# A graph layer with a segment maximum: layernorm's PSUM readings behind the remainder, five shared groups instead of four, 390 rows per partition

## The chip, the cores and the metric

The kernel runs on one core of one Trainium2 chip. The time is the device time of one execution in microseconds, as a median of runs. A profile of one further execution shows each engine's instructions. The engines are called PE (matrix multiplication; PEld is its weight loading), DVE (vector), ACT (activation, reads and writes elementwise), POOL (which here mostly issues gathers) and SP (which issues plain transfers). Each engine works through its own list of instructions in order.

## The reference

There are 6250 nodes with 128 features, and 206,250 edges, sorted by their destination `dst`: 100,000 random ones in both directions, and one from each node to itself.

```python
h = jnp.maximum(_layernorm(x, axis=-1), 0.0)
x_i, x_j = h[dst], h[src]
msg = jnp.concatenate([x_i, x_j - x_i], axis=-1) @ W.T + b
out = jax.ops.segment_max(msg, dst, num_segments=x.shape[0])
return x + jnp.where(jnp.isfinite(out), out, 0.0)
```

The message is a sum of a term of the destination and a term of the source: with W in two halves W1 and W2, it is h[dst] (W1 - W2) + b, plus h[src] W2. So the kernel makes two products per node, and per destination it needs the maximum of the source term over its edges.

## The kernel before

**Tables.** A node's number is l * 50 + q, with l from 0 to 124 and q from 0 to 49. The 50 sets of nodes with one q are called groups; one group is 125 rows of the source term and fits PE's rows. The layernorm stage takes two groups at a time, in 25 steps. For step k, `turn(k)` transposes the normalized rows on PE and copies them to `hT` on ACT; `product(k)` multiplies them into a PSUM tile `pm` (L544, L547) and then reads it twice on ACT: L549 writes a rounded copy to `Bp[:, 0]`, L550 writes both products to a staging area in `acc`. `remainder(k)` subtracts the rounded copy on PE in the same PSUM tile (L556) and reads what is left to `Bp[:, 1]` (L558), so that two matmuls with rounded tables give the full precision. After each fifth step the staging area is written to memory: the table `Bt` by SP (L562), and the destination's term added into the output by POOL (L563). The PSUM tiles named `pm` share two places (`ps_m`, L272), and so do the tiles that `spread_0` (L753) and `spread_a` (L766) take. A tile's place can be taken again only when the last instruction that reads it has run.

The list `micro` (L565) holds the parts of the 25 steps in order: turn k, remainder k-2, product k-1. `ln(n)` (L572) emits the next n of them; `ln_spare` emits as many as a budget of PE time allows, during the counting below.

**Which edges go where.** Each of the 128 partitions holds the edges of 49 destinations. For up to one edge per destination and group, the maximum is taken by one-hot matmuls on PE: the main loop. Groups of the order 41 to 0 have one place per destination. Four pairs of groups are shared: a pair has two places per destination (`MG = 4`), and each place costs two chunks, one of each group of the pair, since the edge in it may come from either. There are 50 places, 8 of them with two chunks: 58 chunks for every tile of destinations. Edges that find no place are the rest: they are compacted to a list per partition, and their rows are gathered from `Bt`, one row for all 128 partitions at a time, GR = 396 rows. A partition with too many hands some to the next one (up to 136); if that isn't enough a flag is set, and a branch at the end goes through all edges one by one (L1188).

**The stage ahead of the loop.** DVE compares each edge with up to 41 neighbours to count its place (L636; PE adds the comparisons up in the PSUM tile `dup`), until 88 us. ACT turns the counts to signs (L721), DVE sums them (L743), and eleven passes of conditional copies (`pass_`, L779, called in L855) compact the list. After pass i the functions in `rest[i]` are emitted. They are: `spread_0` and `spread_a`, by which the partitions' counts go through PE (L754), DVE (L758 to L764) and PE again (L768), and `spread_b`, in which DVE reads the outcome (L772 to L777); what is left of layernorm, `ln(30)` ahead of the passes and the rest after pass 0; `names()`, which reads `dup` on ACT in four pieces (L737) and makes a second operand (L738); `turned()`, which transposes three tables by PE into `dup` and casts them by ACT (L796), each in two parts of 8 and 6 blocks; `clear_early`, two memsets on POOL (L835) in the space of the staging area; and after pass 7 the first gathers and the first one-hots (`build`, L205).

**The main loop.** 13 tiles of destinations (12 of 490, one of 392) by 25 pairs of places: 325 steps. In each, PE makes z for the next pair (L990), ACT turns z to one-hots (L991), PE multiplies them with both tables of `Bp` (L1127, two matmuls a chunk), and DVE takes the maximum (L1134 in a tile's first step, L1136 in the others). Three PSUM tiles hold z, two hold the products. The order of the pairs is made in L977: 8 of the 25 have a place with two chunks. Between, DVE takes in the gathered rows (`stream_step`, L172) and builds the one-hots of later tiles (L205, L209, L212). When a row is due is set by `fill_in` (L1040): GR rows over 291 steps by time estimates of each engine. POOL issues a gather (L92) for each row, up to 36 rows ahead. After the last row the remaining rows of each destination are gathered and merged (L1096 to L1101), in the last 34 steps.

Of the kernel before, what the change touches and what calls it, by code (L numbers as in the profile page):

```python
# [14 lines left out]
AF = mybir.ActivationFunctionType  # L15
# [4 lines left out]
P = 128  # L20
# [9 lines left out]
WIN = 1792  # L30
NBLK = WIN // P
# [4 lines left out]
OV = 136  # L36
GR = 396
R0 = 32
# [7 lines left out]
CNT = 12  # L46
MG = 4
SQ = 64
# [9 lines left out]
def gnn_kernel(tc, x, src, dst, W, b, out):  # L58
# [20 lines left out]
    A_ = nc.scalar  # L79
    T_ = nc.tensor  # L80
# [20 lines left out]
    with ExitStack() as ctx:  # L101
# [14 lines left out]
        with ExitStack() as body:  # L116
            body.enter_context(tc.manual_schedule())
            keep = body.enter_context(tc.tile_pool(name="keep", bufs=1))
            identb = keep.tile([P, P], BF16, name="identb")
# [148 lines left out]
            with ExitStack() as pre:  # L268
# [269 lines left out]
                def where(k):  # L538
                    g, o = divmod(2 * k, GQ)
                    return g % 2, o  # L540

                def product(k):
                    pm = steps[k]["pm"] = ps_m.tile([P, 2, 2 * C], F32, name="pm")
                    T_.matmul(pm[:L], bsel, brow.rearrange("k (o c) -> k o c", o=1).to_broadcast([P, 2, 2 * C]),  # L544
                              start=True, stop=False)
                    for j in range(2):
                        T_.matmul(pm[:L, j], hT[k % 2][:, j, :L], wT, start=False, stop=j == 1)  # L547
                    g, o = where(k)
                    A_.copy(Bp[:L, 0, 2 * k:2 * k + 2], pm[:L, :, :C])  # L549
                    A_.copy(stage[:, g, :, o:o + 2].rearrange("l b q c -> l q b c"),  # L550
                            pm[:L].rearrange("l q (b c) -> l q b c", b=2))
# [14 lines left out]
                for k in range(NP_ + 2):  # L566
                    for f, n in ((turn, k), (remainder, k - 2), (product, k - 1)):
                        if 0 <= n < NP_:
                            micro.append((n if f is turn else -1, lambda f=f, n=n: f(n),
                                          {turn: 0.25, product: 1.15, remainder: 0.13}[f]))  # L570

# [150 lines left out]
                dups = s16.bitcast(BF16)  # L722
                ln(30)
                for r in range(2):
# [8 lines left out]

                def names():
                    for a in range(0, WIN, 512):
                        z = min(a + 512, WIN)
                        A_.copy(dups[:, a:z], dup[:, a:z])  # L737
                    A_.activation(name, q16, AF.Abs)  # L738

# [49 lines left out]

                def turned(t, *todo):  # L790
                    pt = dup.rearrange("p (j l) -> p j l", l=P)
                    for a, z in ((0, 8), (8, NBLK)):
                        for j in range(a, z):
                            for m, (e, w) in enumerate(todo):
                                T_.matmul(pt[:, j], e[:, j * P:(j + 1) * P], w, start=m == 0, stop=m == len(todo) - 1)
                        A_.copy(t[:, :, a:z], pt[:, a:z].rearrange("p j l -> p l j"))  # L796

# [45 lines left out]
                rest = {i: [] for i in range(12)}  # L843
                rest[0] += [spread_0, lambda: ln(len(micro)), names]
                rest[1] += [lambda: turned(TD, (dlc, identb))]
                rest[2] += [spread_a, lambda: turned(TV, (vm, identb), (low, negL))]
                rest[3] += [lambda: turned(TQ, (dups, sgI), (name, halfI))]
                rest[4] += [spread_b]
                rest[5] += [clear_early, load_first]
# [51 lines left out]
            with ExitStack() as main:  # L901
# [74 lines left out]
                for k in range(Q // 2):  # L976
                    order.append([twos.pop(0) if k % 3 == 1 and twos else ones_.pop(0), ones_.pop(0)])  # L977
                assert not twos and not ones_
# [279 lines left out]
```

## Time and profile before

| | us |
|---|---|
| median of 3 runs (777.7 to 780.37) | 779.11 |
| the profiled execution | 781.03 |
| its span, from the first to the last instruction | 779.3 |
| DVE busy in the span | 703.4 |
| PE busy in the span | 684.6 |
| ACT busy in the span | 553.7 |
| POOL busy in the span | 489.7 |
| PE's granted clock, mean | 0.964 |

A row of the profile's timeline has the start in us from the span's start, the duration, engine, line, operation, and the tile written `<-` those read; `xN` stands for N instructions merged to one row. In brackets is how long the engine was idle ahead of it and what ended that. Matmuls overlap, so that the spacing of their starts, and not the mean duration, tells what one costs. A table by stretches gives the busy time of each engine in a part of the span, and PE's granted clock as a share of full speed.

### The profile page before, as it was taken

The numbers are of one execution on the slowest core, as the hardware profiler recorded it, in microseconds if no ns is written. First come the engines' busy times: TensorE is split into PE (matmuls) and PEld (weight loads), VectorE is DVE, ScalarE is ACT, GpSimd is POOL, SyncE is SP. The second block draws the span as 40 slices with busy tenths as digits, with TensorE's granted clock in tenths as the row PEclk, the third lists the DMA queues.
The fourth block names the chain that finished last, engine by engine and source line by source line (L and its number), as shares of the span: only waits on it lengthen the run. The fifth ranks groups of instructions, "written<-read, shape, count | busy, mean of one in ns | idle before, by whom it ended". The sixth has DMA issues, their size and how long they took to land.

```text
span 779.3 us, 12126 instructions
## 1 busy us (share of the span) xinstructions
PE 684.6 (88%) x3776; PEld 517.3 (66%) x3782; DVE 703.4 (90%) x1256; ACT 553.7 (71%) x1162; POOL 489.7 (63%) x519
## 2 busy tenths in 40 slices
PE   0689875678999999999899999999999999989995
PEld 0345454556677676777667777777777777767894
DVE  7999965988999899999999999999999999886885
ACT  4689455275978879888686766868676686855863
POOL 4000011577777777777777777777777777775472
PEclk9999997579999999999999999999999999999998
DMA  6843054023433333433343333334333343332137
GB/s 194 263 100 65 2 116 97 18 82 94 109 107 91 103 111 93 122 92 112 84 119 96 103 110 97 109 107 112 100 105 108 89 125 92 109 103 81 40 77 141
DMA packets 79651, 79.40 MB, mean 102 GB/s; under 512 B 10042, under 2 KB 68495, under 8 KB 79579
## 3 DMA queue, kind: packets, MB, share of 16 engines
q0 software_dynamic: 16560, 37.64, 19.2%
q1 hardware_dynamic: 62667, 40.30, 17.9%
q10 hardware_dynamic: 352, 0.61, 0.3%
q8 instruction: 31, 0.51, 0.3%
q14 instruction: 41, 0.34, 0.1%
HBM read 39.25 MB, written 39.19 MB: 101 GB/s over the span
## 4 chain that ended last, share of the span: by engine, by line
PE 43%; DVE 20%; ACT 17%; issue 10%; DMA 7%; POOL 2%; SPq 0%; DVEq 0%; POOLq 0%; ACTq 0%
PE ps L1127 22%; PE z L990 10%; ACT oh L991 9%; DVE acc L1136 6%; PE pv L244 6%; DMA X<-Bt,ridx 5%; DVE T L636 3%; DVE X L172 3%; ACT Vb L259 2%; PE pm L547 1%; ACT Vf L259 1%; ACT dump L1166 1%; DVE dwin L673 1%; ACT acc L550 1%; POOL X L92 1%
## 5 line engine op out<-in xcount | busy, mean ns | idle before, releaser
L92 POOL DMA_INDIRECT X<-Bt,ridx x396 | 409.6, 1034 | 128.3 <-issue 37.8
L991 ACT ACTIVATE oh<-z 126x490 fp32r<-126x490 f32 (+1 forms) x754 | 380.9, 575 | 146.4 <-PE z L990 143.5
L1127 PE MATMUL ps<-oh,Bp 126*128 126x490 f32 (+1 forms) x1508 | 445.4, 423 | 10.0 <-DVE acc L1136 9.7
L1136 DVE TENSOR_TENSOR acc<-acc,ps 128x980 f32<-128x980 f32 (+1 forms) x312 | 360.1, 1154 | 39.9 <-PE ps L1127 35.5
L1127 PEld LDWEIGHTS ps<-oh,Bp 126*128 126x128 f32 x1508 | 286.0, 192 | 87.0 <-DVE acc L1136 19.2
L990 PE MATMUL z<-Vb,Sel 128*126 128x490 f16 (+1 forms) x650 | 198.0, 373 | 13.8 <-ACT oh L991 7.7
L172 DVE SCALAR_TENSOR_TENSOR X<-X,slim 128x128 f32<-128x128 f32 x395 | 136.1, 345 | 4.0 <-issue 2.4
L990 PEld LDWEIGHTS <-Sel 128*126 128x126 f16 x754 | 99.7, 140 | 48.3 <-issue 14.9
L244 PEld LDWEIGHTS <-OHQ 128*128 128x128 bf16 x840 | 58.7, 161 | 23.2 <-issue 22.5
L563 POOL DMA_DIRECT2D out_x<-acc x10 | 8.8, 1016 | 101.8 <-ACT hT L530 70.2
L244 PE MATMUL pv<-OHD,OHQ 128*128 128x28 bf16 (+1 forms) x826 | 62.0, 228 | 9.5 <-DVE OHD L212 9.5
L92 POOL DMA_INDIRECT R<-M,last_e x49 | 48.0, 980 | 22.3 <-issue 11.3
L205 DVE TENSOR_TENSOR OHQ<-T,IQ 128x1092 bf16<-128x1092 bf16 (+5 forms) x96 | 57.4, 601 | 0.2 <-DVE badc L898 0.2
L990 PE MATMUL z<-Vf,Sel 128*126 128x490 f16 (+1 forms) x104 | 38.7, 373 | 0.5 <-ACT Vf L259 0.5
L625 PE MATMUL dup<-T,identb 128*128 128x512 bf16 (+1 forms) x159 | 36.7, 357 | 2.1 <-DVE T L636 1.0
L1166 ACT ACTIVATE dump<-lane_dl,nbias 128x472 bf16<-128x472 int32 x50 | 35.2, 704 | 0.1
L625 PEld LDWEIGHTS <-identb 128*128 128x128 bf16 x164 | 16.1, 99 | 19.2 <-issue 5.1
L547 PE MATMUL pm<-wT,hT 128*125 128x256 f32 x100 | 26.5, 388 | 0.0
L673 DVE COPY_PREDICATED dwin<-big,dwin 128x472 int32<-128x472 int32 (+10 forms) x12 | 21.9, 1826 | 0.4
L549 ACT CAST Bp<-pm 125x256 fp32r<-125x256 f32 x25 | 9.3, 371 | 18.0 <-PE pm L547 17.8
L636 DVE TENSOR_TENSOR T<-KA,KB 128x1792 bf16<-128x1792 int16 x21 | 21.1, 1081 | 0.0
L547 PEld LDWEIGHTS pm<-wT,hT 128*125 128x125 f32 x100 | 19.3, 193 | 2.7
(301 smaller groups left out, 503.4 us busy)
## 6 DMA issues: line engine op xcount, KB each, us to landing
M<-X SPq DMA_DIRECT2D x66, 384.0 KB
X<-Bt,ridx POOLq DMA_INDIRECT x396
X<-in_x SPq DMA_DIRECT2D x5, 560.0 KB
out_x<-X SPq DMA_DIRECT2D x5, 560.0 KB
Bt<-acc SPq DMA_DIRECT2D x5, 560.0 KB
out_x<-acc POOLq DMA_DIRECT2D x5, 560.0 KB
ownb<-Bt SPq DMA_DIRECT2D x11, 245.0 KB
out_x<-R POOLq DMA_DIRECT2D x5, 480.0 KB
```

Source lines behind the costliest of these rows:

```text
L92: i = G_.indirect_dma_start(out=o, out_offset=None, in_=table, in_offset=bass.IndirectOffsetOnAxis(ap=idx, axis=0))
L172: step = V.scalar_tensor_tensor(G[:, j], state["prev"], slim[:, k:k + 1], G[:, j], op0=ALU.min, op1=ALU.max)
L205: return V.tensor_tensor(OHQ[:, :nl, a:z], over(TQ, z - a), iq, ALU.is_equal)
L244: last = T_.matmul(o, w, m, start=False, stop=True, skip_group_check=True)
L547: T_.matmul(pm[:L, j], hT[k % 2][:, j, :L], wT, start=False, stop=j == 1)
L625: T_.matmul(dup[:, a:z], w, e[:, a:z], start=first, stop=last)
L636: V.tensor_tensor(e, KA[:, 64:], i1, ALU.is_equal)
L990: T_.matmul(z[:L + 1, :n], Sel[:, order[i // 2][j]], f[t % 2][:, :n], start=True, stop=True)
L991: A_.activation(oh[:, :n], z[:L + 1, :n], AF.Relu)
L1127: T_.matmul(ps[:, j, :n], w, o[:, :n], start=m == 0, stop=m == len(todo) - 1)
L1136: V.tensor_tensor(a, a, ps[:, :, :n], ALU.max)
L1166: A_.activation(dump, lane_dl, AF.Sign, scale=2.0, bias=nbias[:, c:c + 1], accum_out=ends[:, c:c + 1])
```

## The change

It has three parts.

1. `product(k)` keeps only its matmuls. Its two ACT readings become `copies(k)`. The order in `micro` is now turn k, product k-1, remainder k-2, copies k-1, with the same budget for a step.
2. What layernorm has left after the counting is emitted in other places. Ahead of the passes there are 16 parts instead of 30; after pass 0 `spread_0`, then 20 parts, with the four pieces of `dups` and `name` behind each four of them; after pass 1 `spread_a`, then the rest in fours, with the first four of the six halves of `turned` behind them; the last two halves come after pass 2, `spread_b` after pass 3 (before: pass 4, and `spread_a` after pass 2).
3. Five pairs of groups are shared (`MG = 5`): 10 of 50 places have two chunks, 60 chunks for each tile; pairs k with k % 5 of 1 or 3 get them. GR falls from 396 to 390.

```diff
-GR = 396
+GR = 390
-MG = 4
+MG = 5
...
                     for j in range(2):
                         T_.matmul(pm[:L, j], hT[k % 2][:, j, :L], wT, start=False, stop=j == 1)
+
+                def copies(k):
+                    pm = steps[k]["pm"]
                     g, o = where(k)
                     A_.copy(Bp[:L, 0, 2 * k:2 * k + 2], pm[:L, :, :C])
...
-                    for f, n in ((turn, k), (remainder, k - 2), (product, k - 1)):
+                    for f, n in ((turn, k), (product, k - 1), (remainder, k - 2), (copies, k - 1)):
                         if 0 <= n < NP_:
                             micro.append((n if f is turn else -1, lambda f=f, n=n: f(n),
-                                          {turn: 0.25, product: 1.15, remainder: 0.13}[f]))
+                                          {turn: 0.25, product: 1.15, remainder: 0.13, copies: 0.0}[f]))
...
-                ln(30)
...
-                def names():
-                    for a in range(0, WIN, 512):
-                        z = min(a + 512, WIN)
-                        A_.copy(dups[:, a:z], dup[:, a:z])
-                    A_.activation(name, q16, AF.Abs)
+                def kept(a):
+                    z = min(a + 512, WIN)
+                    A_.copy(dups[:, a:z], dup[:, a:z])
+
+                def rest_of(cycles, *ops):
+                    for i in range(cycles):
+                        ln(4)
+                        if i < len(ops):
+                            ops[i]()
+
+                rest_of(4)
...
-                def turned(t, *todo):
+                def turned(t, h, *todo):
                     pt = dup.rearrange("p (j l) -> p j l", l=P)
-                    for a, z in ((0, 8), (8, NBLK)):
-                        for j in range(a, z):
+                    a, z = ((0, 8), (8, NBLK))[h]
+                    for j in range(a, z):
...
-                rest[0] += [spread_0, lambda: ln(len(micro)), names]
-                rest[1] += [lambda: turned(TD, (dlc, identb))]
-                rest[2] += [spread_a, lambda: turned(TV, (vm, identb), (low, negL))]
-                rest[3] += [lambda: turned(TQ, (dups, sgI), (name, halfI))]
-                rest[4] += [spread_b]
+                both = [(t, h, todo) for t, todo in ((TD, ((dlc, identb),)), (TV, ((vm, identb), (low, negL))),
+                                                     (TQ, ((dups, sgI), (name, halfI)))) for h in (0, 1)]
+                rest[0] += [spread_0, lambda: rest_of(5, *[lambda a=a: kept(a) for a in range(0, WIN, 512)],
+                                                      lambda: A_.activation(name, q16, AF.Abs))]
+                rest[1] += [spread_a, lambda: rest_of(-(-len(micro) // 4), *[lambda t=t, h=h, todo=todo: turned(t, h, *todo)
+                                                                            for t, h, todo in both[:4]])]
+                rest[2] += [lambda t=t, h=h, todo=todo: turned(t, h, *todo) for t, h, todo in both[4:]]
+                rest[3] += [spread_b]
...
-                    order.append([twos.pop(0) if k % 3 == 1 and twos else ones_.pop(0), ones_.pop(0)])
+                    order.append([twos.pop(0) if k % 5 in (1, 3) and twos else ones_.pop(0), ones_.pop(0)])
```

More of the change, by code (lines that the diff above doesn't have):

```diff
@@ L788, in pass_ @@
                     return step
-                def turned(t, *todo):
+                def turned(t, h, *todo):
                     pt = dup.rearrange("p (j l) -> p j l", l=P)
-                    for a, z in ((0, 8), (8, NBLK)):
-                        for j in range(a, z):
-                            for m, (e, w) in enumerate(todo):
-                                T_.matmul(pt[:, j], e[:, j * P:(j + 1) * P], w, start=m == 0, stop=m == len(todo) - 1)
-                        A_.copy(t[:, :, a:z], pt[:, a:z].rearrange("p j l -> p l j"))
+                    a, z = ((0, 8), (8, NBLK))[h]
+                    for j in range(a, z):
+                        for m, (e, w) in enumerate(todo):
+                            T_.matmul(pt[:, j], e[:, j * P:(j + 1) * P], w, start=m == 0, stop=m == len(todo) - 1)
+                    A_.copy(t[:, :, a:z], pt[:, a:z].rearrange("p j l -> p l j"))
                 own_n = pool.tile([P, 4], F32, name="own_n")
```

## The prediction

> **What bounds the kernel now.** I read the page first, for the size of each kind of work: columns are line, engine, operation, count, busy us, mean ns of one, then idle time before it.
>
> ```profile
> span 779.3 us, 12126 instructions
> ...
> L92 POOL DMA_INDIRECT X<-Bt,ridx x396 | 409.6, 1034 | 128.3 <-issue 37.8
> L991 ACT ACTIVATE oh<-z 126x490 fp32r<-126x490 f32 (+1 forms) x754 | 380.9, 575 | 146.4 <-PE z L990 143.5
> L1127 PE MATMUL ps<-oh,Bp 126*128 126x490 f32 (+1 forms) x1508 | 445.4, 423 | 10.0 <-DVE acc L1136 9.7
> L1136 DVE TENSOR_TENSOR acc<-acc,ps 128x980 f32<-128x980 f32 (+1 forms) x312 | 360.1, 1154 | 39.9 <-PE ps L1127 35.5
> ```
>
> Then the table by stretches (length, then busy us of PE, PEld, DVE, ACT, POOL; clock; DMA), one row for the layernorm stretch and one for three tiles of the main loop, and the first instruction of DVE in tiles 6, 9, 10 and 11.
>
> ```profile
> 89.20:125.20 36.00, 24.16 (x112) 17.37 (x111) 25.70 (x27) 22.22 (x56) 4.04 (x5) 1.00 0.36 73
> ...
> 457.40:595.30 137.90, 132.74 (x752) 102.63 (x751) 132.23 (x218) 99.53 (x195) 106.21 (x105) 1.00 0.38 105
> ```
>
> ```profile
> 455.68 1.18 DVE L1134 TENSOR_TENSOR acc<-ps,acc 128x980 f32<-128x980 f32 x1
> ...
> 593.66 1.18 DVE L1134 TENSOR_TENSOR acc<-ps,acc 128x980 f32<-128x980 f32 x1
> ...
> 639.35 1.18 DVE L1134 TENSOR_TENSOR acc<-ps,acc 128x980 f32<-128x980 f32 x1
> ...
> 687.52 1.18 DVE L1134 TENSOR_TENSOR acc<-ps,acc 128x980 f32<-128x980 f32 x1
> ```
>
> The main loop is bound by PE and DVE together: of 137.9 us PE idles 5.2 and DVE 5.7, in turns. Three tiles take 137.98 us, 46.0 each; tile 10 takes 48.17. Before the loop another thing rules. The timeline of DVE:
>
> ```profile
> 104.01 1.09 DVE L672 TENSOR_SCALAR big<-dwin 128x1788 int32<-128x1788 int32 x1
> ...
> 114.83 0.28 DVE L758 TENSOR_SCALAR rows<-pm 1x128 f32<-1x128 f32 x1 [7.41 <-PE pm L754]
> ...
> 116.65 1.07 DVE L672 TENSOR_SCALAR big<-dwin 128x1784 int32<-128x1784 int32 x1
> ...
> 131.83 0.16 DVE L772 CAST cols__105<-pm 128x1 int32<-128x1 f32 x1 [8.45 <-PE pm L768]
> ...
> 142.81 2.55 DVE L205 TENSOR_TENSOR acc<-T,IQ 128x1092 bf16<-128x1092 bf16 x4 [0.22 <-issue]
> ```
>
> DVE, which has the compaction passes to do, stands still for 7.41 and 8.45 us because two small matmuls (L754, L768) are queued on PE behind layernorm rounds. The chain of waits shows one such round, and the timeline of ACT its third reading:
>
> ```profile
> 94.66 0.38 PE pm L556
> 95.04 0.23 PE pm L544
> 95.27 0.88 PE pm L547 x4
> 96.17 0.23 ACT Bp L549
> 96.44 0.60 ACT acc L550
> ...
> 97.09 0.39 PE pm L556
> ```
>
> ```profile
> 95.08 0.37 ACT L558 CAST Bp<-pm 125x256 fp32r<-125x256 f32 x1 [0.20 <-PE pm L556]
> ```
>
> A round takes 97.09 - 94.66 = 2.43 us; the remainder matmul L556 waits for the readings L549 and L550 of the product just before it. Fourteen rounds run behind 89.2.
>
> **Layernorm's order, and its places (first part of the change).** The new order on PE is turn, product, remainder; the remainder of step k-2 now waits for readings made a round earlier. What is late next: the product needs the PSUM tile of two steps back, free when that step's L558 has ended. From product to product that is 1.11 (L544, L547) + 0.42 (L556 to L558) + 0.37 + 0.04 = 1.94 us; ACT's four readings, some 1.5 us, fit. Gain 0.49 a round, if nothing else enters.
>
> The places enter. The tile of L754 takes one of the two PSUM tiles. One product is always unread at that point, so the next product gets the tile of L754, and that is given back by DVE's L758, behind pass 1. PE therefore stops from about 98 until DVE has done two passes:
>
> - Four rounds end at 97.3; L754 runs at 97.6.
> - L758 comes at 104.0 (where 104.01 starts pass 2 now) and no longer waits. Its group takes 1.82, as from 114.83 to 116.65.
> - PE goes on at 104.3: five rounds, one or two at half clock (below), to 115.6; then L768, to 116.6. ACT's readings of dups and name (rows below) lie between: a quarter of 1.85 in each of four rounds' slack, the 1.74 beside L768.
> - DVE does passes 2 and 3 until 112.7, waits 4.0 for L768, then 0.6 for its group; passes 4 to 7 end at 130.6 (5 to 7 fill 132.4 to 142.4 now, 3.3 each).
> - PE starts the last five rounds at 117.1, with four of the six turned halves among them; each half adds a cast of 0.8 to 1.0 on ACT (L796), so a round takes 2.4 to 3. Last readings at 130.0, last two halves at 134.
>
> ```profile
> 125.23 1.85 ACT L737 CAST s<-dup 128x512 bf16<-128x512 f32 x4
> 126.93 1.74 ACT L738 ACTIVATE d<-q 128x1792 bf16<-128x1792 bf16 x1
> ...
> 141.51 0.81 ACT L796 CAST T<-dup 128x768 bf16<-128x768 f32 x1 [1.52 <-PE dup L795]
> ```
>
> So L205 starts at 134.1 and not at 142.81: **-8.7 us**. Of 15.9 us of waits some 4 stay, and 3.4 become a wait for the last cast (141.51 now, just ahead of L205). SP's writes of the table Bt move with the readings, and POOL is queued behind a memset:
>
> ```profile
> 124.78 1.66 POOL L563 DMA_DIRECT2D out_x<-acc  x2 [11.23 <-ACT acc L550]
> ...
> 134.24 0.75 POOL L835 MEMSET acc<- 128x784 bf16 x1 [6.71 <-DMA out_x<-acc]
> 142.87 1.62 POOL L92 DMA_INDIRECT X<-Bt,ridx  x1 [7.88 <-DVE ridx L828]
> ```
>
> ```profile
> 124.52 0.76 SPq L562 DMA_DIRECT2D Bt<-acc  x2
> 128.07 0.32 SPq L838 DMA_DIRECT2D swin<-Bt  x1
> ```
>
> The memset comes 9.5 us behind the last transfer's issue, which moves from 124.8 to 130.1; the first gather can start at 140.4, 2.4 us earlier. SP's last write of Bt, issued at 130.0, is in by 133.6, since L838, which reads it, starts 3.6 behind it now: it holds up nobody. The order during the counting, ahead of 88, I cost at nothing: DVE is busy there without a break. If that cover were gone, PE has the same 0.49 a round to give, not to lose.
>
> The clock must be watched. Two windows of the table by stretches:
>
> ```profile
> 121.74:125.15 3.41, 1.86 (x7) 1.26 (x8) 1.64 (x1) 1.74 (x5) 0.37 (x1) 1.00 0.00 0
> 125.15:128.56 3.41, 1.01 (x8) 0.85 (x8) 0.00 (x0) 3.41 (x7) 2.38 (x3) 0.50 0.94 218
> ```
>
> PE busy for 55% of a stretch of 3.4 us is followed by a granted clock of 0.50. The pause from 98 to 104 holds nearly two such stretches, so the first round behind it runs slowly; I have put in 1.3 us. [...]
>
> **Two more chunks in each tile.** 13 tiles get 60 chunks for 58: 26 more L990, 26 more L991, 52 more L1127. PE's price is its pitch, not the 423 ns:
>
> ```profile
> 337.27 1.05 PE L244 MATMUL pv<-OHD,OHQ 128*128 128x28 bf16 x14
> ...
> 340.12 0.58 PE L990 MATMUL z<-Vb,Sel 128*126 128x490 f16 x2
> ...
> 340.36 1.69 PE L1127 MATMUL ps<-oh,Bp 126*128 126x490 f32 x6
> ...
> 341.89 0.58 PE L990 MATMUL z<-Vb,Sel 128*126 128x490 f16 x2
> ```
>
> Eight matmuls from 340.12 to 341.89: 0.22 each, 0.66 a chunk, 1.3 us a tile, 17 us in all. Per tile PE has 174 x 0.22 = 38.3, five groups like that of 337.27 (5.2 at most), under 1 for the rest: 44 of 46.0. So 2 us of slack meets 1.3 us of work. Bounds: 0 (all of it fits) and 1.3 (none). Slack that comes in turns is not all usable; I take 0.5 in tiles 1 to 10, 0.7 in tile 0, and the whole price in the last two, where rows end and PE alone is the bound (1.3, and 1.0 for 392 columns): **+8.0**. ACT's 26 x 0.575 = 15 us lie in its idle 146. [...]
>
> **Six rows less.** POOL is full: gathers follow one another at 1.25 us, and near the end DVE waits for them:
>
> ```profile
> 689.76 0.94 POOL L92 DMA_INDIRECT X<-Bt,ridx  x1 [0.31 <-DMA X<-Bt,ridx]
> ...
> 691.00 0.94 POOL L92 DMA_INDIRECT X<-Bt,ridx  x1 [0.30 <-DMA X<-Bt,ridx]
> ```
>
> ```profile
> 682.82 0.35 DVE L172 SCALAR_TENSOR_TENSOR X<-X,slim 128x128 f32<-128x128 f32 x1 [2.37 <-issue]
> ```
>
> DVE saves 6 x 0.35 = 2 us, spread over the tiles and already in the 0.5. The wait of 2.37 is why tile 10 takes 2.2 us over the usual 46.0, and some 1 us more is lost behind it. POOL's chain shortens by 6 x 1.25 + 2.4 = 9.9; the loop reaches the last row about 5 to 6 earlier, so gathers are no longer last: **-3** (0 to -4).
>
> **Sum:** -8.7 + 8.0 - 3 = -3.7. The profiled execution took 781.03 (its span 779.3 and 1.7 around it), 1.9 above the median of 779.11; the sum gives 777.3 there and 775.4 for the median.
>
> **The rivals.**
> - *PE is the bound in every tile.* The price of 17 us is paid in full from the first tile on, because the slack is of a kind that a third chunk cannot use: -8.7 + 16.6 - 3 = +4.9, 784.0, slower. It decides once less than about 0.6 us a tile is hidden. For it: PE busy 96%; against it: DVE busy as much, and the pitch leaves 2 us.
> - *The pause costs the clock.* PE stays at 0.50 over four or five rounds and the turned halves (a round then about 3.2 instead of 1.94, so 4 to 5 us): sum near +0.5, 779.5. For it: 0.50 from 125 on. [...]
> - *No pause.* The tile of L754 does not hold up the next product. Rounds run through; casts and passes both end near 127: -15 + 8 - 3, 769.
> - *The change lacks rows.* If 390 were too few, the test would send the kernel into its edge-by-edge branch, far slower. Counting random edges (32 per dst, 50 groups) five groups of two hold 7 rows per partition more than four, so the margin grows by one: 0.02.
>
> **How the numbers follow.** Forecast 0.45, PE bound 0.20, clock 0.23, no pause 0.10, lack 0.02. A measurement of this kernel tells 0.3% (2.3 us) from no change. The forecast's own spread (gain 6 to 11, chunks 5 to 11) leaves a little of it within 0.3%, and the clock case lies mostly there: faster 0.54, same 0.26, slower 0.20. The likeliest is 775.4; the range takes in both outer cases with a price, 768.5 to 784.0.
>
> **What would show it.** L758 without a wait near 104; PE idle from 98 to 104 with 0.50 behind it; L772 waiting about 4; L205 at 134; first gather at 140; a usual tile of 46.5; no wait of L172 near 683. Wrong would be a tile of 47 or more, an L205 later than 138, or PE without that pause.

## The result, and the profile after

| | before | after |
|---|---|---|
| median, us | 778.75 (777.7 to 780.37) | 769.24 (768.03 to 770.2) |
| ratio, 95% interval | | 0.9873 [0.9858, 0.9888] |
| span of the profiled execution, us | 779.3 | 767.7 |
| end of the first accumulation of the loop, us | 166.8 | 160.4 |
| from there to the last accumulation, us | 604.0 | 599.0 |

The change made the kernel 1.3% faster, 9.5 us; 3.7 had been forecast. The sign and the range (768.5 to 784.0) hold the result, the size doesn't. The loop was to be 5 us longer and is 5 us shorter. Between the line numbers of before and after lie 3 from L549 on, 8 around L760 and 11 in the loop: L1127 is now L1138, L1136 is L1147.

The page of after, the groups that answer to those shown of before:

```profile
span 767.7 us, 12292 instructions
...
L92 POOL DMA_INDIRECT X<-Bt,ridx x390 | 393.2, 1008 | 118.7 <-DMA X<-Bt,ridx 37.8
...
L1138 PE MATMUL ps<-oh,Bp 126*128 126x490 f32 (+1 forms) x1560 | 454.6, 420 | 2.6 <-DVE acc L1147 2.6
...
L1147 DVE TENSOR_TENSOR acc<-acc,ps 128x980 f32<-128x980 f32 (+1 forms) x312 | 360.0, 1154 | 42.4 <-PE ps L1138 39.5
...
L172 DVE SCALAR_TENSOR_TENSOR X<-X,slim 128x128 f32<-128x128 f32 x389 | 133.9, 344 | 0.0
```

PE's products L1138 are 52 more and cost 9 us more of busy time, but the idle time ahead of them fell from 10.0 to 2.6, and the row steps at L172 wait for nothing any more.

Its timeline ahead of the loop, PE, then DVE:

```profile
99.90 0.38 PE L762 MATMUL pm<-ident,nres 128*1 128x128 f32 x2 [0.25 <-ACT Bp L561]
106.20 0.79 PE L544 MATMUL pm<-brow,bsel 128*125 128x512 f32 x1 [5.92 <-DVE rows L766]
```

```profile
105.88 0.26 DVE L766 TENSOR_SCALAR rows<-pm 1x128 f32<-1x128 f32 x1
...
118.12 0.16 DVE L780 CAST cols__105<-pm 128x1 int32<-128x1 f32 x1 [3.65 <-PE pm L776]
...
136.09 1.36 DVE L205 TENSOR_TENSOR acc<-T,IQ 128x1092 bf16<-128x1092 bf16 x2 [3.80 <-ACT T L804]
```

The reader is to see the three things that the prediction named, each 1 to 2 us late: PE stands still for 5.9 us because the small product L762 holds one of the two places of `pm` until DVE comes to L766; DVE's two waits of 7.41 and 8.45 us are now none and one of 3.65; and L205, which opens the loop's work, starts at 136.1 instead of 142.81.

The loop, in the table by stretches (length, then busy us of PE, PEld, DVE, ACT, POOL; clock; DMA), tiles 6 to 8 and tile 10, first of before, then of after:

```profile
456.90:594.80 137.90, 132.74 (x752) 102.63 (x751) 132.23 (x218) 99.53 (x195) 106.12 (x105) 1.00 0.38 105
640.50:688.70 48.20, 45.11 (x245) 34.42 (x243) 44.11 (x74) 33.19 (x65) 37.09 (x37) 0.96 0.37 105
```

```profile
451.10:587.40 136.30, 135.50 (x770) 105.95 (x769) 131.32 (x217) 102.33 (x201) 104.61 (x104) 1.00 0.38 106
632.90:678.30 45.40, 45.13 (x260) 35.33 (x259) 43.81 (x73) 34.11 (x67) 34.78 (x35) 1.00 0.39 110
```

Three tiles hold 18 more matmuls, PE is busy 2.8 us longer, and yet they are 1.6 us shorter: of 5.2 us in which PE stood idle, 0.8 are left. Tile 10 is 2.8 us shorter. The waits between 400 and 665 us (total, count, longest), before and then after, name what PE no longer waits for:

```profile
PEld ps L1127 <- DVE acc L1136: 9.1, 12, 1.2
...
PE pv L244 <- DVE OHD L212: 4.9, 6, 0.9
PE ps L1127 <- DVE acc L1136: 4.5, 9, 0.7
```

```profile
PEld ps L1138 <- DVE acc L1147: 2.2, 7, 0.9
...
PE ps L1138 <- DVE acc L1147: 0.5, 1, 0.5
```

### The profile page after: what moved, and what is told of

It reads as the page before. It is cut to its first block, busy times and chain, and to the rows that moved or that the text cites. A ratio compares the mean times of both kernels' runs of the same rounds, so it can differ in the third digit from the quotient of the medians.

```text
span 767.7 us, 12292 instructions
## 1 busy us (share of the span) xinstructions
PE 692.2 (90%) x3860; PEld 527.1 (69%) x3860; DVE 699.8 (91%) x1250; ACT 564.7 (74%) x1188; POOL 474.4 (62%) x513
## 4 chain that ended last, share of the span: by engine, by line
PE 59%; ACT 19%; DVE 14%; issue 4%; DMA 3%; SPq 0%; DVEq 0%; ACTq 0%; POOLq 0%; POOL 0%
PE ps L1138 32%; PE z L1001 15%; ACT oh L1002 11%; PE pv L244 6%; DVE T L639 3%; ACT Vf L259 2%; DMA X<-Bt,ridx 2%; ACT Vb L259 2%; DVE acc L1147 2%; PE pm L547 1%; DVE stats L402 1%; ACT dump L1177 1%; DVE dwin L676 1%; DMA T<-in_dst 1%; PE pv L1107 1%
## 5 line engine op out<-in xcount | busy, mean ns | idle before, releaser
L1002 ACT ACTIVATE oh<-z 126x490 fp32r<-126x490 f32 (+1 forms) x780 | 393.6, 575 | 129.4 <-PE z L1001 126.0
L92 POOL DMA_INDIRECT X<-Bt,ridx x390 | 393.2, 1008 | 118.7 <-DMA X<-Bt,ridx 37.8
L1138 PE MATMUL ps<-oh,Bp 126*128 126x490 f32 (+1 forms) x1560 | 454.6, 420 | 2.6 <-DVE acc L1147 2.6
L1147 DVE TENSOR_TENSOR acc<-acc,ps 128x980 f32<-128x980 f32 (+1 forms) x312 | 360.0, 1154 | 42.4 <-PE ps L1138 39.5
L1138 PEld LDWEIGHTS ps<-oh,Bp 126*128 126x128 f32 x1560 | 295.1, 191 | 74.5 <-issue 8.6
L1001 PE MATMUL z<-Vb,Sel 128*126 128x490 f16 (+1 forms) x650 | 196.0, 370 | 14.8 <-ACT oh L1002 8.4
L1001 PEld LDWEIGHTS <-Sel 128*126 128x126 f16 x780 | 102.9, 139 | 53.0 <-issue 17.8
L172 DVE SCALAR_TENSOR_TENSOR X<-X,slim 128x128 f32<-128x128 f32 x389 | 133.9, 344 | 0.0
L205 DVE TENSOR_TENSOR OHQ<-T,IQ 128x1092 bf16<-128x1092 bf16 (+5 forms) x96 | 57.2, 599 | 0.2 <-DVE badc L909 0.2
L1001 PE MATMUL z<-Vf,Sel 128*126 128x490 f16 (+1 forms) x130 | 49.0, 377 | 0.5 <-ACT Vf L259 0.5
L547 PE MATMUL pm<-wT,hT 128*125 128x256 f32 x100 | 28.3, 409 | 0.0
L544 PE MATMUL pm<-brow,bsel 128*125 128x512 f32 x25 | 13.2, 528 | 11.1 <-DVE rows L766 5.9
```

Source lines behind the costliest of these rows:

```text
L92: i = G_.indirect_dma_start(out=o, out_offset=None, in_=table, in_offset=bass.IndirectOffsetOnAxis(ap=idx, axis=0))
L172: step = V.scalar_tensor_tensor(G[:, j], state["prev"], slim[:, k:k + 1], G[:, j], op0=ALU.min, op1=ALU.max)
L205: return V.tensor_tensor(OHQ[:, :nl, a:z], over(TQ, z - a), iq, ALU.is_equal)
L1001: T_.matmul(z[:L + 1, :n], Sel[:, order[i // 2][j]], f[t % 2][:, :n], start=True, stop=True)
L1002: A_.activation(oh[:, :n], z[:L + 1, :n], AF.Relu)
L1138: T_.matmul(ps[:, j, :n], w, o[:, :n], start=m == 0, stop=m == len(todo) - 1)
```

## The experiments

Eighteen runs of ten kernels. "Two-chunk pairs" are the loop's steps that have a place with two chunks. Tiles are counted from 0; their lengths run from one tile's last accumulation to the next one's. "Loop" runs from the first accumulation's end to the last one's, in the profiled execution. Ratios go against the kernel before on the same chip.

| kernel | median us | ratio, 95% interval | L205 at | first accumulation | tiles 5 to 9, mean | tile 10 | tile 11 | loop |
|---|---|---|---|---|---|---|---|---|
| before | 778.75 | | 142.8 | 166.8 | 45.9 | 48.2 | 47.6 | 604.0 |
| after | 769.24 | 0.9873 [0.9858, 0.9888] | 136.1 | 160.4 | 45.4 | 45.4 | 45.3 | 599.0 |
| after again | 769.32 | 0.9872 [0.9846, 0.9898] | 135.6 | 159.9 | 45.4 | 45.5 | 45.4 | 597.3 |
| layernorm part alone | 777.86 | 0.9969 [0.9951, 0.9987] | 134.4 | 158.7 | 45.9 | 50.9 | 48.0 | 608.4 |
| loop part alone | 777.83 | 0.9979 [0.9963, 0.9995] | 143.6 | 167.6 | 45.4 | 45.4 | 45.4 | 599.8 |
| loop part, 396 rows | 778.17 | 0.9990 [0.9967, 1.0012] | 143.0 | 167.0 | 45.4 | 45.5 | 45.3 | 601.1 |
| after, spread's tiles in the tile `dup` | 776.65 | 0.9959 [0.9936, 0.9982] | 141.4 | 165.4 | 45.4 | 45.5 | 45.3 | 599.7 |
| after, pairs side by side | 777.05 | 0.9953 [0.9934, 0.9972] | 135.3 | 159.5 | 46.1 | 46.2 | 44.9 | 606.5 |
| layernorm part, other places for eight pairs | 771.03 | 0.9879 [0.9843, 0.9914] | 135.0 | 159.6 | 44.8 | 52.6 | 46.7 | 601.7 |
| after, L766 earlier, other places for ten pairs | 762.89 | 0.9779 [0.9748, 0.9811] | 131.7 | 156.2 | 45.5 | 45.4 | 44.4 | 596.1 |

**390 rows without the fifth group** (the kernel before, with one line of the change).

```diff
-GR = 396
+GR = 390
```

> 390 rows alone, with four shared pairs. Supply theory: the wait for gathers near 683 goes and tile 10 falls from 48.2 to 46: 775 to 776, other tiles as before. If rows held the whole loop and not its end: every tile shorter by 0.5, 771 to 773.

316,049.67 us, and both theories miss: the flag was set and the branch at the end went through all edges one by one (its step, L1208, ran 206,250 times). So the rival "the change lacks rows" describes a real mechanism, and the six rows can only go together with the fifth group; the parts of 390 rows were not to be had alone.

**The layernorm part alone** (the changed kernel with these lines of before):

```diff
-GR = 390
+GR = 396
-MG = 5
+MG = 4
-                    order.append([twos.pop(0) if k % 5 in (1, 3) and twos else ones_.pop(0), ones_.pop(0)])
+                    order.append([twos.pop(0) if k % 3 == 1 and twos else ones_.pop(0), ones_.pop(0)])
```

> The changed kernel with parts of 396 rows, four groups of two chunks and their old order: the layernorm part of the change alone. Absorbing theory: the part ahead of the loop gains what it gains in the changed kernel (L205's first cast at 136 to 138 us instead of 142.8, first accumulation 6.4 us earlier), and a tile still takes 45.7 to 46.5 us, since nothing of the loop is changed: 772 to 774 us, ratio 0.991 to 0.994. Supply theory: the loop before is held by the gathers, whose first starts only 0.9 us earlier; without the six rows the head start is lost again later, as waits of L172 or longer tiles: 776 to 779. Clock theory on the 2.3 us later end of the counting: if the wait of the one-hot cast at L658 for PE near 55 us with a half clock in the window before it comes back, it belongs to the order of the readings; if the count ends near 90.6 us, it was the phase of the clock's windows.

777.86 us, 0.9969. The start came, more of it than in after: the first accumulation 8.1 us earlier (158.7 against 166.8). The loop gave 4.4 back, 2.7 of it in tile 10, which takes 50.9 us, since gathered rows are late (another 1.2 are in tile 0, for which no cause is shown). The timeline of DVE in tile 10 has three waits that aren't in before, beside the one of 2.33 us that before has too (2.37):

```profile
646.48 0.35 DVE L172 SCALAR_TENSOR_TENSOR X<-X,slim 128x128 f32<-128x128 f32 x1 [0.61 <-DMA X<-Bt,ridx]
666.40 0.35 DVE L172 SCALAR_TENSOR_TENSOR X<-X,slim 128x128 f32<-128x128 f32 x1 [0.98 <-DVE acc L1147]
669.30 0.35 DVE L172 SCALAR_TENSOR_TENSOR X<-X,slim 128x128 f32<-128x128 f32 x1 [1.47 <-DMA X<-Bt,ridx]
```

The loop starts 8 us earlier, the first gather only 2.5 us earlier (140.4 against 142.9), so the rows' reserve shrinks by the difference. The supply theory holds for this part alone.

**The loop part alone, and the same with 396 rows** (before, with the changed lines the other way round; the second without the change of GR):

> The kernel before with parts of 390 rows, five groups of two chunks and the new order of pairs: the loop's part alone. Absorbing theory: the two extra chunks of a tile go into PE's 1.6 us of idle time, and the six rows less take some 0.4 us a tile off DVE, so a usual tile takes 45.4 us with PE idle for 0.3 us of it, and the loop is 4 to 6 us shorter: 773 to 776 us, ratio 0.993 to 0.996. Price theory (0.66 us a chunk and three us for the rows): 783 to 785, ratio 1.006. Supply theory: as much of the gain as the rows bring, 2 to 4 us.

> The kernel before with five groups of two chunks and the new order, parts of 396 rows kept: the chunks alone. Absorbing theory: PE's 1.6 us of idle time a tile take the 1.3 us of extra products, DVE's work is the same and its edge is not: 45.7 to 46.1 us a tile, 778 to 782 us, ratio 1.000 to 1.004. Price theory: 0.66 us a chunk, 8 us in all: 786 to 788, ratio 1.010 or more. Order theory: if the even spacing of the two-chunk pairs is what took the idle time out, this kernel is faster than before even with 396 rows: 774 to 777.

777.83 (0.9979) and 778.17 us (0.9990). The first has the tile and the loop of the absorbing theory (45.4 us, 4.2 us shorter), but its time lies 1.8 above the range. With 396 rows the usual tile is 45.4 us, just as in after, so the chunks and their places did it and not the rows. The price theory falls: with 26 chunks more the loop was 2.9 us shorter, and with six rows less 1.3 more (601.1 to 599.8). The time fits the absorbing theory and not the order theory (774 to 777), but the tile went lower than the absorbing theory had (45.7 to 46.1), which left the order open. The page's group of L172, before, then the layernorm part alone, then this kernel with 396 rows, shows where tiles 10 and 11 gained:

```profile
L172 DVE SCALAR_TENSOR_TENSOR X<-X,slim 128x128 f32<-128x128 f32 x395 | 136.1, 345 | 4.0 <-issue 2.4
```

```profile
L172 DVE SCALAR_TENSOR_TENSOR X<-X,slim 128x128 f32<-128x128 f32 x395 | 136.8, 346 | 6.6 <-DMA X<-Bt,ridx 3.2
```

```profile
L172 DVE SCALAR_TENSOR_TENSOR X<-X,slim 128x128 f32<-128x128 f32 x395 | 136.9, 347 | 0.0
```

With all 396 rows the waits for them are gone: the last gather is issued at 701.8 instead of 711.0. The page's group of the gathers in this kernel shows where that time comes from:

```profile
L92 POOL DMA_INDIRECT X<-Bt,ridx x396 | 398.6, 1007 | 128.4 <-issue 35.3
```

The same 396 gathers took 409.6 us in before (1034 ns each), so they are 11.0 us shorter in sum, enough for the 9.2 by which the last one comes earlier. Why a gather gets shorter I haven't found; the program's plan of when rows are due is made with the chunks' times, and was not changed by itself.

**The changed kernel once more**, beside the kernel that is told of next:

> The changed kernel once more. Two halves theory: the early start alone lost 6 us again in the loop, where rows came late in tiles 10 and 11, and the chunks and rows alone began late; together the early start is kept: 768 to 770 us, ratio 0.986 to 0.989. Chip theory: the first result was better by its chip; 772 to 776, near the product of the two single ratios (0.995). The first cast of L205 is at 136 if L658 waits for PE near 55 us again (the phase of the clock's windows), at 134 if not.

769.32 us, 0.9872, the first result again. L205 starts at 135.6, between the two values expected: L658 waits only 0.18 us here, but the counting itself began 0.8 us later than in the first profile. The two parts alone would make 0.9969 x 0.9979 = 0.9948; together they make 0.9872, 6 us more. Of these, 4.4 are what the loop gave back in the layernorm part alone; for the 2.7 of tile 10 it is the rows' reserve that the loop part brings that lets the earlier start last. The rest is near the scatter of these executions (below).

**Where the two-chunk pairs lie.** Eight pairs, no chunk added, against the layernorm part alone:

```diff
-                    order.append([twos.pop(0) if k % 3 == 1 and twos else ones_.pop(0), ones_.pop(0)])
+                    order.append([twos.pop(0) if k % 3 == 0 and twos else ones_.pop(0), ones_.pop(0)])
```

> The layernorm part alone (396 rows, four groups of two chunks), with its eight two-chunk pairs at the first, fourth, seventh place of a tile and so on, instead of the second, fifth, eighth. Spacing theory: PE's two waits in a tile, at the first and the thirteenth pair, meet two-chunk pairs now and go; PE's idle time falls from 1.6 to under 0.8 us and a tile takes 44.4 to 45.1 us, less than with five groups (45.45). Work theory: PE's 44.0 us and DVE's 43.8 are too near each other, the waits appear at other pairs, and a tile takes 45.5 to 46.2, as in the layernorm part alone (45.7).

771.03 us, 0.9879. The spacing theory holds in the tiles, which the first accumulation of tile 6 and of tile 9 show, first in the layernorm part alone (137.99 us apart), then here (134.69):

```profile
448.77 1.18 DVE L1145 TENSOR_TENSOR acc<-ps,acc 128x980 f32<-128x980 f32 x1
...
586.76 1.18 DVE L1145 TENSOR_TENSOR acc<-ps,acc 128x980 f32<-128x980 f32 x1
```

```profile
446.00 1.18 DVE L1145 TENSOR_TENSOR acc<-ps,acc 128x980 f32<-128x980 f32 x1
...
580.69 1.18 DVE L1145 TENSOR_TENSOR acc<-ps,acc 128x980 f32<-128x980 f32 x1
```

```profile
447.20:581.90 134.70, 132.22 (x753) 102.77 (x752) 131.66 (x217) 98.93 (x195) 103.29 (x104) 1.00 0.39 106
626.70:679.20 52.50, 45.34 (x237) 33.50 (x235) 44.47 (x73) 32.94 (x65) 40.22 (x41) 0.97 0.37 101
```

The same work, 132.2 us of PE and 131.7 of DVE, fits into 134.7 us instead of 138.0, 1.1 a tile. The program plans DVE's row steps by the order of the pairs, so that they move too: "places" means both, and no run parts them. The gathers are shorter here too (1010 ns against 1025, the last one issued at 699.9 instead of 705.7), with four groups: so that isn't the fifth group's alone. The second row is tile 10: 52.5 us, 7.7 more than a usual one, since L172 waits for rows; on this kernel's page:

```profile
L172 DVE SCALAR_TENSOR_TENSOR X<-X,slim 128x128 f32<-128x128 f32 x395 | 135.9, 344 | 6.9 <-DMA X<-Bt,ridx 3.6
```

The faster the tiles, the sooner the rows run out. Even so this kernel, without a fifth group, is within a few us of the changed one: 771.03 against 769.32 on one chip.

Ten pairs, side by side, against the changed kernel:

```diff
-                    order.append([twos.pop(0) if k % 5 in (1, 3) and twos else ones_.pop(0), ones_.pop(0)])
+                    order.append([twos.pop(0) if k % 5 in (1, 2) and twos else ones_.pop(0), ones_.pop(0)])
```

> The changed kernel with the two two-chunk pairs of every five side by side (second and third). Work theory: 45.4 to 45.6 us a tile, 768 to 771 us. Spacing theory: PE's idle time over 1 us a tile, 46.2 us a tile or more, 776 us or more.

777.05 us, 0.9953: the time of the spacing theory, not its sign. A tile takes 46.1, and PE idles only 0.45 us of it; instead its busy time is longer for the same number of matmuls. Tiles 6 to 8, the changed kernel run again and this one:

```profile
448.80:585.20 136.40, 135.64 (x772) 106.00 (x771) 131.43 (x217) 102.37 (x201) 104.39 (x106) 1.00 0.39 106
```

```profile
454.10:592.40 138.30, 136.96 (x771) 105.61 (x770) 132.36 (x216) 102.56 (x201) 106.02 (x106) 1.00 0.39 105
```

DVE idles 5.9 us in three tiles instead of 5.0. So places decide with ten pairs too, by 0.7 us a tile; what delays PE's matmuls within its busy time there stays open.

**The pause of PE.** The changed kernel, with the spread's two small tiles in columns added behind those of `dup`:

```diff
-                dup = ps_d.tile([P, WIN], F32, name="dup")
+                dup = ps_d.tile([P, 2048], F32, name="dup")
-                    spread["n"] = ps_m.tile([P, 512], F32, name="pm")
+                    spread["n"] = dup[:, WIN:]
-                    p = spread["c"] = ps_m.tile([P, 512], F32, name="pm")
+                    p = spread["c"] = dup[:, WIN + P:]
```

> The changed kernel, with the two small tiles of the spread (row counts and columns) in the spare end of the bank of dup instead of one of the two places that the products of layernorm use. Place theory: PE's pause of 5.9 us before the product at 106 us goes, with the half clock behind it; the last cast of L205 moves from 136 to 129 to 132, and the time falls by 3 to 6 us from that of the changed kernel: 763 to 766 us. Supply theory: the first gather stays near 142 and the loop, held by the gathers at first, gives the time back: 768 to 770. Dependency rival: the spread's products wait for the readers of dup instead, and nothing is gained: 768 to 771.

776.65 us: the dependency rival, and dearer than it had said. PE's pause is gone, but the timeline of DVE has another wait:

```profile
127.43 0.16 DVE L780 CAST cols__105<-dup 128x1 int32<-128x1 f32 x1 [10.89 <-ACT T L804]
...
141.36 2.55 DVE L205 TENSOR_TENSOR acc<-T,IQ 128x1092 bf16<-128x1092 bf16 x4 [0.19 <-issue]
```

L780 now waits 10.89 us until ACT has cast the last half of the last table out of `dup` (L804, 126.59 to 127.40), and with it stand the passes. This cast reads other columns of `dup` than L780. What L780 reads comes from the products L776, whose last operand was written by 109.8 (L772, 109.57 and 0.22); the profile names L804 and not L776 as what ended the wait. Whether the dependency is kept for the whole tile `dup` or for a part of it, no run tells.

The other way is to shorten the time that the place is held: DVE's steps L766 to L772 one pass earlier, the second products where they were. It ran undisturbed only together with other places for the ten pairs (first and third of every five):

```diff
+                def spread_c():
                     p = spread["c"] = ps_m.tile([P, 512], F32, name="pm")
...
-                rest[0] += [spread_0, lambda: rest_of(5, *[lambda a=a: kept(a) for a in range(0, WIN, 512)],
+                rest[0] += [spread_0, spread_a, lambda: rest_of(5, *[lambda a=a: kept(a) for a in range(0, WIN, 512)],
...
-                rest[1] += [spread_a, lambda: rest_of(-(-len(micro) // 4), *[lambda t=t, h=h, todo=todo: turned(t, h, *todo)
+                rest[1] += [spread_c, lambda: rest_of(-(-len(micro) // 4), *[lambda t=t, h=h, todo=todo: turned(t, h, *todo)
...
-                    order.append([twos.pop(0) if k % 5 in (1, 3) and twos else ones_.pop(0), ones_.pop(0)])
+                    order.append([twos.pop(0) if k % 5 in (0, 2) and twos else ones_.pop(0), ones_.pop(0)])
```

> The changed kernel with the vector steps of the spread's first part one pass earlier, and the two-chunk pairs at the first and third place of every five. Place theory: L205's first cast at 131 to 133 instead of 135 to 136; work theory: tiles 5 to 10 stay at 45.2 to 45.5 us, tiles 1 to 4 fall by up to 0.7 each: 763 to 766 us, ratio 0.979 to 0.983. Row rival: tiles 10 and 11 wait for rows (L172 idle over 2 us): 768 to 770.

762.89 us, 0.9779: below both kernels. The timeline of PE, and that of DVE (here L780 is L781):

```profile
101.85 0.50 PE L544 MATMUL pm<-brow,bsel 128*125 128x512 f32 x1 [2.62 <-DVE rows L766]
```

```profile
101.53 0.26 DVE L766 TENSOR_SCALAR rows<-pm 1x128 f32<-1x128 f32 x1
...
113.79 0.16 DVE L781 CAST cols__105<-pm 128x1 int32<-128x1 f32 x1 [0.20 <-PE pm L777]
131.67 1.96 DVE L205 TENSOR_TENSOR acc<-T,IQ 128x1092 bf16<-128x1092 bf16 x3 [3.72 <-ACT T L805]
```

The pause is 2.6 us, DVE's wait for the second products has gone too, and L205 comes 4 us earlier than in after. The other places brought nothing in tiles 5 to 9 (45.5 us), as the work theory said, and 47.5 in tiles 1 to 3, against 47.6; tiles 0 and 11 are shorter (47.3 and 44.4). So most of the gain is the start's, and the rows kept up.

**Runs that tell nothing of these theories.** Ten of the eighteen runs stand in three groups in which every kernel, the one before too (965.2, 957.99 and 968.92 us), took 23 to 24% longer than elsewhere, with engines waiting for nothing that the trace shows. An example is PE's weight loads at L1001 (us in total, times, longest), first in the changed kernel there, then in its first profile:

```profile
PEld L1001 <- issue: 108.6, 86, 11.9
```

```profile
PEld L1001 <- issue: 17.8, 26, 3.1
```

A kernel's own runs differ by 1 to 5% there, and the effects looked for are below 2%. So no theory is judged by these ratios; all kernels but two were run again, as told above. The one with 390 rows alone, told first, belongs to the first group; its 316,049 us don't hang on a per cent. The others are these, with the edits shown above.

The layernorm part alone, first run:

> Layernorm's part alone: the new order and the new places, with four shared pairs and 396 rows. Supply theory (gathers set when the rows end, near 711 to 718, whatever comes ahead of the loop): the loop starts some 6 us earlier, but the first gather only 1 us earlier, so most of the gain is lost at the last rows: 775 to 777 where before has 779. Stage theory (what is won ahead of the loop stays won): 772 to 773.

1.0012 [0.9914, 1.011]. The loop part alone:

> The loop's part alone: five shared pairs, their order, 390 rows, old layernorm. Slack theory (the two chunks of a tile fit into PE's idle 5 us of 138, the rows relieve the end): 774 to 776, tiles of 45.4. Price theory (a chunk costs its 0.66 us, the gain lies elsewhere): 779 to 784, tiles of 46.5.

1.0132 [1.004, 1.0224]. The loop part with 396 rows:

> Five shared pairs and their order alone, with 396 rows. Slack theory: usual tiles 45.4 to 46.0, the end held by the gathers as before: 777 to 780. Price theory: 26 chunks of 0.66 us, half to all of it: 785 to 793.

1.0205 [1.0105, 1.0305]. The changed kernel:

> The changed kernel once more, beside the next three. Two halves theory: the early start alone (776.1 us of span) lost 6 us again in the loop, where rows came late in the eleventh and twelfth tile, and the chunks and rows alone (775.7) began late; only together is the early start kept, so 768 to 770 us, ratio 0.986 to 0.989, well below the product of the two ratios (0.9969 by 0.9979, 0.995). Chip theory: the first result is that of another chip; here 774 to 777. The wait of L658 for PE near 55 us, which two kernels with the same counting did not show, is absent or there by the phase of the clock's windows: with it the first cast of L205 is at 136, without it at 134.

1.0008 [0.9944, 1.0072]. The changed kernel with L766 to L772 one pass earlier and its pairs in place (the last diff without its change of the order), which was not run again by itself:

> The changed kernel, with the vector steps of the spread's first part (L766 to L772) one pass earlier, right behind the product that they read; the spread's second products stay where they are. Place theory: L766 then runs near 102 instead of 104 to 106, so the place of pm comes free 3 us sooner, PE's pause of 5.9 us falls to 2 or 3 us, layernorm's rounds end 3 us earlier and L205's first cast is at 131 to 133; the time falls by 2 to 4 us, if the rows keep up: 765 to 767. Row theory: first gather and rows are late as before, and tiles 10 and 11 give back what the start gains: 768 to 770.

0.9946 [0.9874, 1.0019]. The pairs side by side, twice:

> The changed kernel with the two two-chunk pairs of every five side by side (second and third) instead of apart (second and fourth), so that three one-chunk pairs follow one another, as they do once a tile in the kernel before. Work theory: PE's work, 45.2 us a tile, is more than DVE's 43.8, DVE keeps a lead, and a tile takes 45.4 to 45.6 us however the pairs lie: ratio as the changed kernel's. Spacing theory: it is the even spacing that removed PE's two waits a tile; with three one-chunk pairs in a row PE waits again for a place in ps, 0.5 us or more at each of five spots: 46.5 us a tile or more, and 10 us or more above the changed kernel.

> The changed kernel with the two two-chunk pairs of every five side by side (second and third) instead of apart (second and fourth). Work theory: PE has 45.2 us of work a tile and DVE 43.8, so DVE keeps a lead however the pairs lie: 45.4 to 45.6 us a tile, 768 to 771 us. Spacing theory: with three one-chunk pairs in a row DVE falls behind and PE waits for a place in ps again: PE's idle time rises from 0.3 to over 1 us a tile, 46.2 us or more, 776 us or more.

1.0 [0.9943, 1.0056] and 0.9976 [0.9936, 1.0016]. The other places for eight pairs:

> The changed kernel with parts of 396 rows and four groups of two chunks, as the layernorm part alone, but its eight two-chunk pairs at the first, fourth, seventh place of a tile and so on, instead of the second, fifth, eighth. The two waits of PE in a tile of that kernel stand at the first pair (for a place in ps) and at the thirteenth (for the one-hot of L212); both are two-chunk pairs now. Spacing theory: PE's idle time falls from 1.6 to under 0.8 us a tile and a tile takes 44.4 to 45.1 us, less than with five groups. Work theory: DVE's 43.8 us and PE's 44.0 are too near each other, waits appear at other pairs, and a tile takes 45.5 to 46.2 as in the layernorm part alone (45.7).

1.0121 [0.9981, 1.0262]. Both edits together, the kernel of the last row of the table:

> The changed kernel with two edits: the vector steps of the spread's first part (L766 to L772) one pass earlier, and the two-chunk pairs at the first and third place of every five instead of the second and fourth. Place theory for the first: L766 runs near 102 instead of 105, PE's pause falls from 5.9 to 2 or 3 us, and L205's first cast is at 131 to 133 instead of 135 to 136. Work theory for the second: PE's 45.2 us of work bound tiles 5 to 10, so they stay at 45.2 to 45.5, and only tiles 1 to 4, where PE still has 1.5 to 2 us of idle time at the first and thirteenth pair, fall by up to 0.7 us each. In sum 3 to 6 us below the changed kernel: 763 to 766 us, ratio 0.979 to 0.983. Row rival: tiles 10 and 11 wait for rows again (L172 idle over 2 us) and give the start's gain back: 768 to 770.

0.9952 [0.99, 1.0004]. Seven of these nine intervals hold 1; what the layernorm part gains ahead of the loop, for one, can't be seen through waits of up to 13.0 us at L1001 in that run.

## Why the prediction was wrong in size

The loop's part of the forecast, by tiles, against what was measured (after less before, us):

| | forecast | measured |
|---|---|---|
| tiles 0 to 9 | +5.2 | -1.2 |
| tiles 10 and 11, where the rows end | -1.2 | -5.0 |
| last tile | +1.0 | +1.25 |

Of the 10.0 us by which the loop was better than forecast, 6.4 lie in tiles 0 to 9 and 3.8 in tiles 10 and 11. The start was 2.0 us worse (L205).

- **Layernorm's order and its places, -8.7: the mechanism right, -6.7 in size.** Rounds of 1.94 us, the pause, the wait for the second products and the wait for the last cast all came. L205 came at 136.1 for 134.1, the first gather at 141.9 for 140.4. First accumulations were 6.4, 6.9, 7.2, 7.3 and 8.1 us earlier in five executions with this start; most of that spread is when the counting ends. In after one wait came in addition, at L658 in the counting, which I had costed at nothing "because DVE is busy there without a break":

```profile
55.77 0.63 DVE L658 TENSOR_SCALAR T<-dlc__197 128x1792 bf16<-128x1792 bf16 x1 [1.85 <-PE dup L628]
```

  PE ran at half clock just there (0.50 from 51.6 to 55.0; next section but one). In the layernorm part alone, and in the changed kernel run again, the same instruction waited 0.18 us; so this isn't the new order's doing.

```profile
53.82 0.63 DVE L658 TENSOR_SCALAR T<-dlc__197 128x1792 bf16<-128x1792 bf16 x1 [0.18 <-PE dup L628]
```

- **Two more chunks in each tile, +8.0: this step failed.** The term counted only what the chunks add, 0.5 us a tile. What it left out is that the same line of the diff moves the two-chunk pairs; I had read that line as only counting the chunks. A usual tile was to be 0.5 us longer and is 0.5 shorter (45.9 to 45.4). Places alone, with no chunk added, are worth 1.1 us a tile (45.9 to 44.8 with eight pairs) and 0.7 with ten; they took out the time in which PE and DVE waited for each other in turns, of which I wrote that it "is not all usable". All but 0.3 us a tile was. A price for the chunks is still there: against the better of the two places for eight pairs that were run, a usual tile costs 0.6 more (45.4 for 44.8), and the last tile took 1.25 more (1.0 forecast). The 5 at the low end of the term's spread (5 to 11) is shown by no run: eight matmuls of the loop took 0.22 us each in before (340.12 to 341.89), and with chunks and places together, 396 rows kept, the loop was 2.9 us shorter. Tiles 1 and 2 are 0.1 shorter, tile 3 is 2.0 longer, for which I have no cause, and tile 4 is 1.1 shorter, where the mean granted clock was 0.97 in before and 1.00 in after.
- **Six rows less, -3: too small, and for a reason that isn't the rows.** Tiles 10 and 11 were 2.7 and 2.3 us shorter. With 396 rows they are so too: these 5.0 us are more than the 2.9 by which that whole loop is shorter; six rows alone are worth 1.3, within the scatter of single executions. The reserve of rows came with the fifth group and its places, from shorter gathers; why these are shorter stays open.
- **The sum.** The three terms were added as if each stood alone. The start's gain doesn't: by itself 4.4 us of 8.1 are lost again in the loop, 2.7 of them in tile 10 to waits for rows.
- **The rivals.** PE as the bound in every tile came in after, with PE idle 0.3 us of 45.4, and still wasn't slower, since the tile became shorter first. The pause cost one round at half clock, 3.2 us for 1.94 (106.2 to 109.4), as put in; PE was busy for 3.36 of the 3.40 us from 106.2 to 109.6, and 1.00 came behind them. "No pause" gave the right time for a wrong reason. The lack of rows is real, but only without the fifth group.

## What to carry to other kernels

Where two engines are busy by 96% each and idle in turns, as here, the order of long and short steps can decide, and more work that comes with better places can cost less than nothing: before pricing such a change, look at which steps the waits stand, and count a move of the long steps as a part of its own. Gains at the start of a stage last only as far as its supply (here the gathered rows) moves with it, so look at the reserve at the far end of the stage. A small result that borrows a place from a running pipeline should be read at once; putting it into a tile that another engine reads for long can be worse, as it was here (10.89 us at L780).

## What the hardware showed beside

In before and in after PE's granted clock changes only at certain times, whole multiples of about 3.41 us apart (in after 51.6, 55.0, 102.8 and 109.6, in before 125.2, 145.6 and 149.1), and they lie elsewhere in each of the two: from 51.6 to 125.2 it is about 21 and a half such steps. In after, the stretch before L658's wait had PE busy for 46%, and the next one was granted 0.50; in the layernorm part alone the same work, 41% busy in the window shown (which is not set by clock changes there), was followed by 1.00:

```profile
48.20:51.60 3.40, 1.58 (x9) 0.67 (x7) 3.40 (x13) 2.90 (x7) 1.86 (x2) 1.00 0.64 187
51.60:55.00 3.40, 3.40 (x10) 2.00 (x8) 2.31 (x4) 3.40 (x9) 0.00 (x0) 0.50 0.97 146
```

```profile
48.00:51.40 3.40, 1.41 (x8) 0.57 (x6) 3.40 (x13) 2.72 (x6) 1.86 (x2) 1.00 0.77 204
51.40:54.80 3.40, 3.35 (x17) 2.03 (x17) 3.09 (x6) 3.40 (x9) 0.00 (x0) 1.00 0.90 140
```

The prediction took 55% busy ahead of 0.50 for the same as an idle stretch. An idle stretch is followed by 0.50 in after (102.8 to 106.2), but the busy share alone doesn't tell: in before 50% came ahead of 1.00 (91.02 to 94.43), 55% ahead of 0.50 (121.74 to 125.15), and 76% ahead of 0.50 (145.63 to 149.04). What in a stretch decides, no run shows.

In tile 4, whose work is the same in after and in the kernel with the spread's tiles in the tile `dup`, the clock differs between the two: 49.8 us at 1.00 in after, 52.5 us at 0.93 there.

```profile
356.30:406.10 49.80, 46.53 (x268) 35.29 (x266) 47.62 (x99) 37.53 (x78) 38.22 (x39) 1.00 0.36 100
```

```profile
359.10:411.60 52.50, 49.22 (x268) 37.19 (x266) 47.70 (x99) 37.54 (x77) 40.31 (x41) 0.93 0.36 97
```

So 2 us at one place and 2.7 at another come and go with the clock between single profiled executions (that the place of these times decides is likely, but not shown), and a step of the sum smaller than that is read from several kernels that share it.
